# Two groups of layer 2 gathered ahead, its seeds and two ranges fetched inside layer 1, and the SBUF pools laid out in another order

## The chip, the cores and the metric

The kernel runs on one core of a Trainium2 chip. The metric is the device time of one execution in microseconds (us); lower is better. Five engines work side by side, each through its own instructions in the order in which they were written: TensorE (PE, with its weight loads as PEld), VectorE (DVE), ScalarE (ACT), GpSimd (POOL) and SyncE (SP). An instruction that waits holds up everything behind it on its engine. SP, ACT and POOL also issue the DMA transfers, so a transfer that must wait for its buffer holds up the later transfers of the same engine.

## The reference

A graph network of two layers over 6250 nodes with 256 features and 100000 edges, then a residual and a layer norm. The edges are sorted by `dst`, and `dst` is skewed to low numbers.

```python
def _gin_agg(h, src, dst, eps, n_nodes):
    agg = jax.ops.segment_sum(h[src], dst, num_segments=n_nodes)
    return (1.0 + eps) * h + agg
...
h = _gin_agg(x, src, dst, eps1, n)          # 256 wide
h = jax.nn.relu(h @ W1a + b1a)              # 256 -> 512
h = jax.nn.relu(h @ W1b + b1b)              # 512 -> 512
h = _gin_agg(h, src, dst, eps2, n)          # 512 wide
h = jax.nn.relu(h @ W2a + b2a)              # 512 -> 512
out = h @ W2b + b2b                         # 512 -> 256
...
x = _layernorm(x + out, axis=-1)
```

## The kernel before

Nodes are cut into 49 tiles of 128 rows (`t`, the last with 106), edges into 782 chunks of 128. The output of layer 1, called `h` in the profile (`h1` in the code), goes to DRAM and is read again by layer 2.

**Two ways to aggregate.** The seven lowest tiles (0 to 6, "heavy") receive the first 288 chunks. For them the kernel counts how often each node feeds each heavy node (`counting`, L1680, L1712, L1897), and multiplies these counts by the features, one *range* of four tiles after another: in layer 1 by `first_products` (L1606), in layer 2 by `second_products`. There a range `r` is read from `h` into `xr` (L1307), split on ACT and DVE into two parts (`upper` L1362, L1363, L1367), its counts are read from DRAM into `ci` (L1387), cast into `cf` by ACT (L1399), and PE multiplies (L1470: eight matmuls of 512 columns for each of seven heavy tiles). There are 13 ranges; the last has only tile 48. The sums collect in `whole_acc`.

The other 494 chunks belong to 85 *groups* of up to 16 chunks. A group's chunks are gathered row by row: one indirect DMA on POOL for each chunk (L488), 128 rows at a time, into one of six *pieces* of four chunks (layer 2: three in `early`, three in `late`). PE adds them up with a selection matrix (L1066), ACT and DVE split the sum (L1108, L1110), PE spreads it over 128 rows (L1119), and DVE adds it into the accumulators of the tiles that the group reaches (L1129). Piece `i` takes the place of piece `i - 6`, so its gathers wait for that piece's L1066.

**Dense part.** When all of a tile's parts are in, it is turned (L1165, L1177) and multiplied by the two weight matrices (L1204, ACT L1214, L1233). Layer 1 then adds the bias (L1243), applies relu (L1245) and stores to `h` (L1246, from ACT). Layer 2 adds the residual, normalises and stores (L1255 to L1285). An accumulator starts as a scaled copy of the tile's own rows, its seed (`seeding`, L1307, L916).

**The order.** Everything is written out once by a small simulator in the kernel (`Plan`): processes ask for an engine with a cost and a priority (a lower number goes first), for a buffer, or for an event, and the order in which the requests are granted is the instruction order of each engine. Layer 1's instructions stand ahead of layer 2's on every engine. `orders` gives the groups: layer 1 runs from the highest group down; tiles 7 and 6 are its last ones.

**The seam of the layers.** Tiles 6 and 7 (`LATE`) are the last to be stored. Layer 2 therefore begins with a group (`FORE`, group 1, twelve chunks) whose gathers read only the rows of `h` ahead of those two tiles; edges that come from tiles 6 and 7 are pointed at an empty row, and `late_edges` counts them and adds them later by two products of counts and rows (L982 to L1008, L1029, the rows in `sown`). All further gathers read the whole of `h` and wait until it is stored. One range (tile 48 alone) of layer 2's products is done inside layer 1, from when the counting is over (`AHEAD2 = 1`).

**Buffers.** SBUF pools are opened one after the other. Layer 1: `first`, `keep1`, `loan1` and `last1`; layer 2: `keep2` and `loan2` in the same place, once the others are closed. A tile of layer 2 waits for the last user of the layer-1 tile whose place it takes. Layer 2's weights (L735 to L737) are the first tiles of `loan2`, and `fetch()` is called at the head of layer 2's program.

The functions that the change touches follow.

Of the kernel before, what the change touches and what calls it, by code (L numbers as in the profile page):

```python
# [17 lines left out]
P = 128  # L18
EPS_LN = 1e-5
GRP = 20  # L20
PARTS = 4
# [25 lines left out]
PASS = 0.00042  # L47
LATE = (6, 8)
HASTE = -14.0
AHEAD2 = 1  # L50
ACCS2 = 4
AFTER = 4.0
# [300 lines left out]
def tile_gin_residual_layernorm(  # L353
# [115 lines left out]
    FORE0, FOREN = groups[FORE][0], len(members[FORE])  # L469
# [7 lines left out]
    def gather(number, i, table, width, *places):  # L477
# [7 lines left out]
        if number == 2 and pieces[number][i][0] == FORE:  # L485
            table, rows_in, first = h1[: GAP + 1, :], fore, FORE0
# [254 lines left out]
    def rows(t):  # L741
        return min(P, N - t * P)
# [25 lines left out]
    def ordered(ctx):  # L768
# [17 lines left out]

        def layer(number, pools, table, width, scale, weights, ba, wide, at=None, aside=None, right=None):
# [5 lines left out]
            keep, loan, last_ = pools  # L793
# [14 lines left out]
            def reach(g):  # L808

                return range(lo[g] if once or SAME else max(lo[g], tiles), hi[g] + 1)  # L810

            last_use, uses = {}, {t: 0 for t in range(NT)}
            for k, g in enumerate(order):
                for t in reach(g):
                    last_use[t] = k
                    uses[t] += 1
            heavy = range(tiles)
            blocks, taken = [], None
            for t in reversed(range(NT)):
                single = last_use.get(t, -1) >= len(order) - ENDING  # L820
                if taken and not single and len(taken) < TILES and (t >= tiles or (tiles - 1 - t) % TILES):
                    taken.insert(0, t)
                else:
                    taken = [t]
                    blocks.append(taken)
                    if single:
                        taken = None
# [22 lines left out]
            def fetch_rows(i):  # L850
                nonlocal pool_free
                if i < len(pieces[number]):
# [5 lines left out]
                    plan.at(pool_free + LANDINGS[number - 1], arrived[i].set)  # L858

# [4 lines left out]
                keep, [P, 2, width], F32 if once else F32R, "split", SPLITS if once else 3  # L864
            )
            zt_room = Tiles(keep, [P, kk, TILES * P], F32, "zt", 2)
            ht_room = Tiles(keep, [P, KH, TILES * P], F32, "ht", 2)
            if once:
                h_room = Tiles(keep, [P, H], F32, "h1r", 3)
            acc_room = Tiles(  # L870
                keep if once else loan, [P, TILES, width], F32, "acc", ACCS if once else ACCS2
            )
            if not once:
                r_room = Tiles(loan, [P, TILES, D], F32, "r", 2)
                mv_room = Tiles(loan, [P, TILES, 2], F32, "mv", 2)
                st_room = Tiles(loan, [P, 6], F32, "st", 3)
                sd_room = Tiles(loan, [P, TILES], F32, "sd", 2)
                rs_room = Tiles(loan, [P, TILES], F32, "rs", 2)

            if not once:  # L880
                apart = loan.tile([P, len(reach(FORE)), width], F32, name="apart")
                assert all(len(blocks[block_of[t]]) == 1 for t in reach(FORE))

            def seeding(bs, want):
                for i, b in enumerate(bs):
# [5 lines left out]
                    if not once and ts[0] in reach(FORE):  # L891
                        token = Place()
                        token.tile = apart[:, ts[0] - lo[FORE] :]
                    else:
                        token = yield ("get", acc_room, 0)
                    a = token.tile
# [1325 lines left out]
```

## Time and profile before

| | |
|---|---|
| median of 3 runs | 1317.04 us (1312.97 to 1320.39) |
| the profiled execution | 1315.43 us, of which the span of its instructions 1313.6 us |
| instructions | 18937 |
| POOL | 955.4 us busy, 73% of the span |
| moved by DMA | 306.27 MB |

The profile is one execution. A row of the timeline has the start in us, the duration, the engine, the line and the operation, tiles written and read, the count, and in brackets the idle time of the engine ahead of it and what ended it. A row of the groups by line has the count, the busy time and the mean in ns of one, and then the engine's idle time before these instructions with what ended it. A row of the chain of waits has start, duration and what the end was waiting for in that time. A row of windows has, for one stretch, the busy time of each engine, the granted PE clock, and the busy share and rate of the DMA engines. "issue" is idle time for which the profile shows no wait.

### The profile page before, as it was taken

Reading aid. Unit: us, or ns where it says so; the run is one execution under the profiler, and the core shown is the slowest. Engines: PE = TensorE matmul, PEld = TensorE weight load, DVE = VectorE, ACT = ScalarE, POOL = GpSimd, SP = SyncE. Lnnn points to the kernel's source line nnn. Section 1 sums busy time; section 2 is a strip of 40 time slices with the busy share of each in tenths; the row PEclk is TensorE's granted clock in tenths of the full one; section 3 lists DMA queues with packets and bytes.
Section 4 is the critical chain, followed back from the end, with each engine's and each line's share of the span. In section 5 each row is a group of like instructions: output and inputs, shape, how many; then the busy total and the mean of one; then the engine's idle time right before and its main releaser. Section 6 shows DMA issues by size and latency. Waiting matters only on the chain.

```text
span 1313.6 us, 18937 instructions
## 1 busy us (share of the span) xinstructions
PE 1183.7 (90%) x6117; PEld 760.0 (58%) x6117; DVE 874.6 (67%) x2070; ACT 619.8 (47%) x1137; POOL 955.4 (73%) x1001
## 2 busy tenths in 40 slices
PE   6869889999898899779859998999899999999986
PEld 4435455555554455345426676777677667677666
DVE  7978986877886776653147877777666665563343
ACT  6217777575657652464254444344244444242212
POOL 6777777777777777777567777777777777777760
PEclk9879999999999999987879999999999999999999
DMA  6446677666667765575889989788889899877771
GB/s 217 149 131 207 203 210 223 183 202 214 204 201 215 223 197 156 172 227 169 257 293 321 326 252 324 238 301 277 301 254 309 292 308 311 281 234 237 240 229 39
DMA packets 161072, 306.27 MB, mean 233 GB/s; under 512 B 25625, under 2 KB 93103, under 8 KB 160964
## 3 DMA queue, kind: packets, MB, share of 16 engines
q0 software_dynamic: 63232, 194.31, 48.0%
q1 hardware_dynamic: 76778, 86.19, 19.9%
q10 hardware_dynamic: 20954, 24.45, 5.2%
q8 instruction: 52, 0.85, 0.3%
q14 instruction: 56, 0.46, 0.1%
HBM read 274.42 MB, written 30.44 MB: 232 GB/s over the span
## 4 chain that ended last, share of the span: by engine, by line
PE 46%; DMA 16%; DVE 12%; POOL 10%; issue 8%; ACT 6%; ACTq 1%; DVEq 1%; SPq 0%; POOLq 0%
PE bank L1204 12%; POOL early L488 9%; PE bank L1233 9%; PE bank L1066 8%; PE bank L1470 8%; DMA early<-in_x_dram,srcs 5%; PE bank L1119 3%; DMA early<-h,places 3%; PE bank L1606 3%; DVE acc L1129 3%; DVE at L1897 2%; DMA late<-h,places 2%; DMA sown<-h 2%; PE bank L1165 2%; PE bank L1712 1%
## 5 line engine op out<-in xcount | busy, mean ns | idle before, releaser
L488 POOL DMA_INDIRECT early<-in_x_dram,srcs x494 | 480.9, 973 | 153.8 <-issue 128.8
L488 POOL DMA_INDIRECT late<-h,places x242 | 232.6, 961 | 79.6 <-issue 60.3
L488 POOL DMA_INDIRECT early<-h,places x240 | 228.6, 952 | 73.1 <-issue 59.7
L1129 DVE SCALAR_TENSOR_TENSOR acc<-bank,mask,acc 128x256 f32<-128x256 f32 (+1 forms) x360 | 206.6, 606 | 65.0 <-PE bank L1119 58.3
L1233 PE MATMUL bank<-w1b_s,ht 128*128 128x512 f32 (+1 forms) x392 | 184.5, 595 | 2.0 <-ACT ht L1214 1.4
L1204 PE MATMUL bank<-zt,w2a_s 128*128 128x256 f32 (+2 forms) x896 | 181.7, 356 | 3.6 <-ACT zt L1177 2.4
L1066 PE MATMUL bank<-early,sel 128*32 128x256 f32 (+1 forms) x1492 | 139.6, 485 | 40.2 <-DMA early<-in_x_dram,srcs 24.4
L1204 PEld LDWEIGHTS bank<-zt,w2a_s 128*128 128x128 f32 x896 | 154.2, 192 | 33.3 <-issue 8.4
L1470 PE MATMUL bank<-upper,cf 128*128 128x512 f32 (+1 forms) x343 | 148.4, 433 | 0.0
L1470 PE MATMUL bank<-xr,cf 128*128 128x512 f32 (+1 forms) x343 | 136.5, 398 | 0.0
L1897 DVE TENSOR_TENSOR at<-bank,at 128x490 f32 x174 | 116.0, 667 | 25.5 <-ACT cf L1555 13.7
L940 DVE TENSOR_TENSOR sel<-iota,slot 128x256 f32<-128x256 f32 (+3 forms) x116 | 50.9, 439 | 106.0 <-PE bank L1066 98.8
L1119 PE MATMUL bank<-split,to 128*128 128x256 f32 (+2 forms) x340 | 105.7, 430 | 10.4 <-ACT split L1100 4.1
L1214 ACT ACTIVATE ht<-bank,b2a_s 128x256 f32<-128x256 f32 (+2 forms) x112 | 44.6, 443 | 147.9 <-PE bank L1204 144.8
L1066 PEld LDWEIGHTS bank<-early,sel 128*32 128x32 f32 x1492 | 39.5, 113 | 127.6 <-issue 85.3
L1233 PEld LDWEIGHTS bank<-w1b_s,ht 128*128 128x128 f32 (+1 forms) x392 | 72.7, 189 | 67.8 <-issue 54.1
L1606 PE MATMUL bank<-xh,cf 128*128 128x512 f32 (+1 forms) x343 | 100.6, 429 | 11.6 <-DVE xh L1534 10.3
L1399 ACT CAST cf<-ci 128x512 fp32r<-128x512 uint16 (+1 forms) x91 | 54.1, 595 | 116.9 <-PE bank L1470 95.0
L1204 PE MATMUL bank<-zt,w1a_s 128*128 128x256 f32 (+2 forms) x432 | 102.4, 386 | 5.4 <-ACT zt L1177 1.7
L1712 PE MATMUL bank<-cb,ca 128*128 128x490 f16 x288 | 89.0, 386 | 14.3 <-DVE at L1897 5.3
L1680 DVE TENSOR_SCALAR cb<-numbers,spot 128x490 f16<-128x490 f16 x288 | 91.2, 358 | 15.7 <-PE bank L1712 15.5
L1233 PE MATMUL bank<-w2b_s,ht 128*128 128x256 f32 (+1 forms) x392 | 100.0, 386 | 0.0
(176 smaller groups left out, 1692.2 us busy)
## 6 DMA issues: line engine op xcount, KB each, us to landing
raw<-in_x_dram SPq DMA_DIRECT2D x48, 512.0 KB
h<-h1r ACTq DMA_DIRECT2D x48, 256.0 KB
xr<-h SPq DMA_DIRECT2D x11, 1024.0 KB
counts<-ci ACTq DMA_DIRECT2D x84, 128.0 KB
ci<-counts SPq DMA_DIRECT2D x84, 128.0 KB
acc<-h SPq DMA_DIRECT2D x18, 512.0 KB
early<-in_x_dram,srcs POOLq DMA_INDIRECT x494
acc<-in_x_dram SPq DMA_DIRECT2D x21, 256.0 KB
```

The costliest lines, as they stand in the source:

```text
L488: nc.gpsimd.indirect_dma_start(out=rows_[:, j, :], out_offset=None, in_=table, in_offset=bass.IndirectOffsetOnAxis(ap=rows_in[:, c - first ...
L1066: mm = nc.tensor.matmul(pm[b * SLOTS : (b + 1) * SLOTS], sel[:, c - groups[g][0], :], rows_[:, l, :], start=(c == part[0]), stop=(c == par ...
L1119: nc.tensor.matmul(pu[:, i * width : (i + 1) * width], to[:used], split[:used, l, :], start=(once or l == 0), stop=(once or l == 1),)
L1129: nc.vector.scalar_tensor_tensor(acc[t], pu[:, i * width : (i + 1) * width], mask[:, t - lo[g], g : g + 1], acc[t], op0=ALU.mult, op1=ALU.add,
L1204: nc.tensor.matmul(ph[:, (f - o) * TILES * P : (f - o) * TILES * P + nb], wa[:, k, f * P : (f + 1) * P], zt[:, k, :nb], start=(k == 0), st ...
L1233: nc.tensor.matmul(po[:m], ht[:, f, i * P : i * P + m], wb[:, f, :], start=(f == 0), stop=(f == KH - 1),)
L1399: nc.scalar.copy(cf_token.tile[:, :n, :].rearrange("p k j -> p (k j)"), token.tile[:, : n * P],)
L1470: nc.tensor.matmul(bank[token.number][:, :width], cf[:m, j, :], of[:m, j, :], start=(j == 0 and of is upper), stop=(j == len(ks) - 1 and o ...
L1606: nc.tensor.matmul(bank[tokens[i].number][:, : 2 * width], cf[:m, j, :], xh[:m, j, :, :].rearrange("p a d -> p (a d)"), start=(k == 0), st ...
L1680: made = nc.vector.tensor_scalar(token.tile, numbers, spot[:, c : c + 1], None, op0=ALU.is_equal)
L1712: mm = nc.tensor.matmul(bank[token.number][:, : NT * W], a.tile[:, c % BATCH, :], b.tile, start=(j == 0), stop=(j == n - 1),)
L1897: nc.vector.tensor_tensor(to, bank[token[0].number][:, : NT * W].rearrange("p (k w) -> p k w", w=W), to, op=ALU.add,)
```

## The change

1. `FORES` takes the place of `FORE`: the first two groups that reach no lower than tile 7 (groups 1 and 2, twelve chunks each, both reaching tiles 7 and 8) are gathered first, from the rows ahead of tiles 6 and 7. `late_edges` runs once for each; `late_rows` fetches tiles 6 and 7 once for both. Its count is now twelve matmuls of 256 columns, a copy, two turns on PE and a second copy, where it was 24 of 32 columns and one copy.
2. `AHEAD2 = 2`: the range of tiles 44 to 47 joins tile 48's inside layer 1. From the planned landing of layer 1's last gather less 1.5 us (`quiet`) until its last dense matmul (`settled`), no new step of this work is granted (`busy`).
3. `first_seeds` reads the seeds of layer 2's first four blocks (`acc2`, now on the right side of SBUF with `whole_acc`) 8 us after the counting is over, and scales them inside layer 1 at the lowest priority. `ci2` has five buffers in place of six.
4. The pools are `first`, `leave`, `hold`, `keep`, `loan` in layer 1, and `leave`, `hold`, `keep` in layer 2. Layer 2's weights and residual tiles stand in `leave2`; `split`, `zt`, `ht` and `apart` in `hold2`; `late`, `sel`, `to`, `cf` and `sown` in `keep2`.
5. Layer 2's weights are fetched at the planned time 5.0 (`SOWN2`) instead of at the head of its program, and `HASTE`, the planned start of its gathers, goes from -14 to -18.

```diff
+SOWN2 = 5.0
+LEAD = 1.5
-HASTE = -14.0
-AHEAD2 = 1
+HASTE = -18.0
+AHEAD2 = 2
+SOW = 8.0
...
-    FORE = next(g for g in range(BEGIN[1], NG) if lo[g] >= max(HEAVY[1], LATE[0]))
+    FORES = [g for g in range(BEGIN[1], NG) if lo[g] >= max(HEAVY[1], LATE[0])][:2]
+    FORETOLD = range(min(lo[g] for g in FORES), max(hi[g] for g in FORES) + 1)
-    orders[2] = [FORE] + [g for g in reversed(range(BEGIN[1], NG)) if g != FORE]
+    orders[2] = FORES + [g for g in reversed(range(BEGIN[1], NG)) if g not in FORES]
...
-        if number == 2 and pieces[number][i][0] == FORE:
+        if number == 2 and pieces[number][i][0] in FORES:
             table, rows_in, first = h1[: GAP + 1, :], fore, FORE0
...
+            quiet, settled, finished = [], Event(plan), []
+
+            def busy():
+                return once and quiet and plan.now >= quiet[0] and not settled.done
...
+                    if once and i == len(pieces[number]) - 1:
+                        quiet.append(pool_free + LANDINGS[number - 1] - LEAD)
...
+            def first_seeds():
+                yield ("rest", SOW)
...
+                for ts in some[:ACCS2]:
+                    for t in ts:
+                        yield ("until", stored[t])
+                    a = begun_with["pool"].tile(
+                        [P, TILES, H], F32, tag="acc2", name="acc2", bufs=ACCS2
+                    )
+                    in_rows(ts, a, h1, place)
...
+                yield ("rest", SEEDS[1])
+                for ts, a in todo:
+                    if busy():
+                        yield ("until", settled)
+                    yield ("on", "ACT", act(len(ts) * H), 6)
...
-                for part in range(PARTS):
-                    yield ("on", "PE", 0.12 * T * h, 1)
-                    for j in range(T):
-                        for i in range(part, n, PARTS):
-                            nc.tensor.matmul(
-                                ap[:, j * P + part * SLOTS : j * P + (part + 1) * SLOTS],
-                                hot[i][:, j * P : (j + 1) * P],
-                                sel[:, members[FORE][i][0] - FORE0, :],
-                                start=(i < PARTS), stop=(i >= n - PARTS),
-                            )
+                yield ("on", "PE", 0.3 + 0.04 * n, 1)
+                for i, (c, part) in enumerate(members[g]):
+                    nc.tensor.matmul(
+                        ap[part * SLOTS : (part + 1) * SLOTS, : T * P], sel[:, c - c0, :], hot[i],
+                        start=(i < PARTS), stop=(i >= n - PARTS),
+                    )
+                flat = b[:, : 2 * T * P].bitcast(F32)
+                yield ("on", "ACT", act(T * P), 1)
+                nc.scalar.copy(flat, ap[:, : T * P])
...
+                for j in range(T):
+                    nc.tensor.transpose(
+                        ap[:, j * P : (j + 1) * P], flat[:, j * P : (j + 1) * P], ident
+                    )
...
+            def late_rows():
                 yield ("rest", max(0.0, 1.0 - plan.now))
-                s_token = yield ("get", sown["room"], 0)
-                in_rows(range(*LATE), s_token.tile, h1, place)
+                token = yield ("get", sown["room"], 0)
+                in_rows(range(*LATE), token.tile, h1, place)
...
+                    finished.append(t)
+                    if len(finished) == NT:
+                        plan.then(settled.set)
...
-            cf_room = Tiles(loan, [P, RANGE, P], F32R, "cf", 4)
+            cf_room = Tiles(loan if once else keep, [P, RANGE, P], F32R, "cf", 4)
...
-                ci_room = Tiles(pool2, [P, RANGE * P], mybir.dt.uint16, "ci2", 6)
+                ci_room = Tiles(pool2, [P, RANGE * P], mybir.dt.uint16, "ci2", 5)
...
+                            if busy():
+                                yield ("until", settled)
                             token = yield ("get", banks, first or 3)
                             yield ("on", "PE", 2 * PASS * len(ks) * width, first or 3)
...
                     second_products(list(reversed(range(len(ranges))))[:AHEAD2])
+                    plan.start(first_seeds())
...
             def fetching():
-                yield ("rest", WEIGHTS)
+                yield ("rest", WEIGHTS if once else SOWN2 - plan.now)
                 fetch()
...
-            pool = [
+            first, leave, hold, keep, loan = (
                 inner.enter_context(tc.tile_pool(name=name, bufs=1))
-                for name in ("first", "keep1", "loan1")
-            ]
+                for name in ("first", "leave1", "hold1", "keep1", "loan1")
+            )
...
-            pool = [
-                inner.enter_context(tc.tile_pool(name=name, bufs=1)) for name in ("keep2", "loan2")
-            ]
-            layer(2, (*pool, None), h1[:, :], H, e1[:, 1:2], second(pool[1]), b2a_s, D)
+            leave, hold, keep = (
+                inner.enter_context(tc.tile_pool(name=name, bufs=1))
+                for name in ("leave2", "hold2", "keep2")
+            )
```

More of the change, by code (lines that the diff above doesn't have):

```diff
@@ L468, in tile_gin_residual_layernorm @@
     }
-    FORE0, FOREN = groups[FORE][0], len(members[FORE])
+    FORE0 = groups[FORES[0]][0]
+    FOREN = sum(len(members[g]) for g in FORES)
+    assert all(len(members[g]) == PARTS * groups[g][1] for g in FORES)
     places2 = const.tile([P, NCP - NC2], I32, name="places2")
@@ L785, in ordered, with layout, reach @@
         begun_with = {}
+        def layout(number):
+            tiles, order = HEAVY[number - 1], orders[number]
+            def reach(g):
+                return range(lo[g] if number == 1 or SAME else max(lo[g], tiles), hi[g] + 1)
+            last_use, uses = {}, {t: 0 for t in range(NT)}
+            for k, g in enumerate(order):
+                for t in reach(g):
+                    last_use[t] = k
+                    uses[t] += 1
+            blocks, taken = [], None
+            for t in reversed(range(NT)):
+                single = last_use.get(t, -1) >= len(order) - ENDING
+                if taken and not single and len(taken) < TILES and (t >= tiles or (tiles - 1 - t) % TILES):
+                    taken.insert(0, t)
+                else:
+                    taken = [t]
+                    blocks.append(taken)
+                    if single:
+                        taken = None
+            return reach, uses, blocks
         def layer(number, pools, table, width, scale, weights, ba, wide, at=None, aside=None, right=None):
@@ L792, in layer @@
             late_ = not once
-            keep, loan, last_ = pools
+            keep, loan, last_, hold, leave = pools
             wa, wb, bias, fetch = weights
@@ L806, in __init__ @@
                     self.make = lambda: pool.tile(shape, dtype, tag=name, name=name, bufs=bufs)
[L808 to L816, printed above, removed]
-            heavy = range(tiles)
[L818 to L827, printed above, removed]
+            reach, uses, blocks = layout(number)
+            heavy = range(tiles)
             block_of = {t: b for b, ts in enumerate(blocks) for t in ts}
@@ L890, in seeding @@
                         yield ("until", want[b])
-                    if not once and ts[0] in reach(FORE):
+                    if not once and ts[0] in FORETOLD:
                         token = Place()
-                        token.tile = apart[:, ts[0] - lo[FORE] :]
+                        token.tile = apart[:, ts[0] - FORETOLD[0] :]
                     else:
@@ L896, in seeding @@
                     a = token.tile
+                    if not once and begun_with["seeds"] and begun_with["seeds"][0][0] == ts:
+                        begun_with["seeds"].pop(0)
+                        held[b] = token
+                        for i, t in enumerate(ts):
+                            acc[t] = a[:, i, :]
+                            ready[t].set()
+                        settle(ts[0])
+                        continue
                     where = natural if once else place
@@ L1032, in adding_late @@
                     )
-                for token in tokens:
-                    token.release()
+                counts_token.release()
+                sown["late"].used()
                 plan.then(plan.start, then)
@@ L1069, in sums @@
                                 start=(c == part[0]),
-                                stop=(c == part[-1] and (once or g != FORE)),
+                                stop=(c == part[-1] and (once or g not in FORES)),
                             )
@@ L1397, in converting @@
                     cf_token = yield ("get", cf_room, 0)
+                    if busy():
+                        yield ("until", settled)
                     yield ("on", "ACT", act(n * P), first or 3)
@@ L1462, in multiplying @@
                             yield ("until", halved[r])
+                            if busy():
+                                yield ("until", settled)
                             token = yield ("get", banks, first or 3)
```

104 lines of the change are left out of this document (69 added, 35 removed).

## The prediction, made before the result was known

> **What bounds the kernel now.** I read the page's engine shares first, then windows along the span, then the gathers in the groups by line.
>
> ```profile
> PE 1183.7 (90%) x6117; PEld 760.0 (58%) x6117; DVE 874.6 (67%) x2070; ACT 619.8 (47%) x1137; POOL 955.4 (73%) x1001
> core 0: us, PE busy (x) PEld busy (x) DVE busy (x) ACT busy (x) POOL busy (x), PEclk, DMA share, GB/s
> 600.00:640.00 40.00, 38.40 (x189) 21.54 (x187) 10.30 (x20) 17.33 (x42) 28.38 (x31) 0.90 0.55 167
> 640.00:661.00 21.00, 15.91 (x62) 9.76 (x62) 1.57 (x3) 4.78 (x13) 9.46 (x10) 0.76 1.00 325
> 661.00:675.00 14.00, 0.63 (x8) 0.36 (x8) 6.79 (x24) 10.52 (x16) 6.25 (x6) 0.68 0.65 204
> 675.00:1200.00 525.00, 512.61 (x2724) 358.84 (x2726) 346.69 (x680) 215.95 (x404) 398.22 (x417) 0.98 0.88 289
> 1200.00:1281.00 81.00, 75.13 (x456) 53.59 (x449) 35.10 (x84) 16.11 (x38) 58.63 (x62) 1.00 0.77 229
> L488 POOL DMA_INDIRECT late<-h,places x242 | 232.6, 961 | 79.6 <-issue 60.3 <-DMA h<-h1r 6.2 <-DMA late<-h,places 5.8
> L488 POOL DMA_INDIRECT early<-h,places x240 | 228.6, 952 | 73.1 <-issue 59.7 <-DMA early<-h,places 7.3 <-PE bank L1066 2.1
> ```
>
> By share PE is the bound. But PE has the products of counts to fill its time with; POOL has nothing but gathers, and its 482 gathers (242 + 240) took 461.2 us with 152.7 us between them, of which only the 6.2 us behind `DMA h<-h1r` are one long wait: the rest is 0.3 us a gather. So from its start on POOL runs at its own pace, and PE's work fits under it. POOL's timeline shows it:
>
> ```profile
> 648.55 0.95 POOL L488 DMA_INDIRECT early<-h,fore  x1 [11.04 <-DMA acc<-h]
> 662.31 0.95 POOL L488 DMA_INDIRECT early<-h,fore  x1 [0.30 <-issue]
> 669.48 1.01 POOL L488 DMA_INDIRECT late<-h,places  x1 [6.22 <-DMA h<-h1r]
> 685.06 0.95 POOL L488 DMA_INDIRECT early<-h,places  x1 [0.30 <-DMA late<-h,places]
> 1276.26 0.95 POOL L488 DMA_INDIRECT late<-h,places  x1 [0.30 <-issue]
> ```
>
> Twelve gathers lie from 648.55 to 662.31, 1.25 us apart; then POOL stands still until tiles 6 and 7 are stored; the 25th gather starts at 685.06, the last at 1276.26. Ahead of 648.55 it idled 11 us for the store of tile 8. Layer 2's end is therefore that start, plus 494 gathers, plus the waits, plus the 37.3 us from 1276.26 to the span's end at 1313.6. A microsecond taken out of POOL's start or its one wait comes off the end, as long as PE keeps up.
>
> **The change part by part.** The sum is made against the profiled execution, 1315.4 us (span 1313.6), which is 1.6 us under the median.
>
> *Second group ahead.* Twelve more gathers no longer ask for tiles 6 and 7. The 25th then starts at 648.55 + 24 x 1.253 = 678.6 instead of 685.06: **-6.4**. The whole of `h` is there by then:
>
> ```profile
> 662.52 6.19 DMA h<-h1r
> 668.90 0.56 DVE L940 TENSOR_TENSOR sel<-iota,slot 128x384 f32<-128x384 f32 x1 [7.08 <-DMA h<-h1r]
> 675.24 5.02 PE L1066 MATMUL bank<-early,sel 128*32 128x512 f32 x24
> 690.95 1.13 PE L1029 MATMUL bank<-sown,zt 128*128 128x512 f32 x2
> 693.79 1.02 PE L1029 MATMUL bank<-sown,zt 128*128 128x512 f32 x2
> ```
>
> The store lands at 662.52 + 6.19 = 668.7. What is late next is the place: the 25th gather takes the first group's first piece, which L1066 freed at 675.24 + 5.02 = 680.3. That matmul waited for `sel`, whose DVE stood 7.08 us behind the store because `sel` lay where layer 1's buffers had been. With the new pools DVE can begin when the last dense matmul ends, near 661, so L1066 should be through by about 673. The price is a second count and 1.13 + 1.02 = 2.2 us of L1029 on PE, hidden under POOL's pace; uncovered it would cost 2.2 plus about 1 us of short matmuls.
>
> *Range 44 to 47 and the seeds.* Seven groups of eight L1470 matmuls leave layer 2:
>
> ```profile
> 747.40 1.87 PE bank L1470 x8
> L1399 ACT CAST cf<-ci 128x512 fp32r<-128x512 uint16 x84 | 51.9, 619 | 115.4 <-PE bank L1470 95.0 <-DMA ci<-counts 9.4 <-issue 6.2
> 662.97 3.23 ACT L916 ACTIVATE acc<-acc,e 128x1024 f32<-128x1024 f32 x3 [0.48 <-ACT h1r L1245]
> ```
>
> 7 x 1.87 = 13.1 us of PE, seven casts x 0.619 = 4.3 us of ACT (77 of 84 remain). Between 600 and 640 PE was idle only 1.6 of 40 us; between 661 and 675 it did 0.63 us in 14. So I expect one to three of the seven ahead of layer 1's end and the rest behind its last dense matmul, where PE stood idle. By itself this takes nothing off POOL's chain (0); it lets PE enter layer 2 some 10 us less behind. The seeds' scaling (3.23 us and one more) leaves an ACT that was not late: 0.
>
> *Layer 1's end.* Here transfers decide:
>
> ```profile
> 311.11 3.46 DMA early<-in_x_dram,srcs
> 636.57 7.26 DMA early<-in_x_dram,srcs
> 634.13 0.38 SPq L735 DMA_DIRECT2D w2a_s<-in_L_gnn_W2a_dram  x1
> 640.56 0.33 ACTq L1246 DMA_DIRECT2D h<-h1r  x1
> 643.97 1.08 PE L1066 MATMUL bank<-early,sel 128*32 128x256 f32 x8 [4.26 <-DMA early<-in_x_dram,srcs]
> 647.71 0.25 SPq L1312 DMA_DIRECT2D acc<-h  x1
> q1 hardware_dynamic: 2795, 3.90, 79.6%
> q0 software_dynamic: 225, 0.59, 11.5%
> ```
>
> The last gather of layer 1 needed 7.26 us, where an undisturbed one took 3.46, and PE idled 4.26 us for it; tile 8's store, which starts layer 2's gathers, took from 640.56 to 647.7. In this stretch (634 to 650, the two queue rows) SP's queue moved 3.90 MB, the weights among them from 634.13 on, and the gathers 0.59. The change moves the weights past the seam and range and seeds ahead of it; what SP still issues here is the next range's rows. A landing like the 3.46 would bring the start forward by 3.7 us (7.1 - 3.46). On the other side each product that slips ahead of tile 8's dense work costs 1.9. Bounds -4 and +4; I take **-2**, since the weights (1.7 MB by their shapes) leave this stretch, but SP's order is not known.
>
> The Trainium skill, "DMA: Bandwidth & Descriptors", section "Queues, rings and completion order", says that each DMA engine serves its queues in turn, a packet at a time. This speaks against putting another range and the seeds beside layer 1's last forty microseconds of gathers; the trace agrees that a full SP queue roughly doubles a landing (7.26 against 3.46). By this rule alone, with SP's queue as full as before at 636, the term would be 0 instead of -2 and the time 1308, still inside the forecast's band below.
>
> *Pools.* `late` may now wait. By the tiles' sizes in the code, the last third of `late` and a strip of the middle lie where layer 1's `cf` was, and `cf` is used until the last product of range 44 to 47. The 17th gather is due at 668.6 and the 21st at 673.6; five products behind 661 end near 661 + 9.4 = 670.4. Nothing to 6.4 us; I take **+0.5**, the trace showing PE and ACT free there.
>
> *Tail.*
>
> ```profile
> 1277.67 0.60 PE L1165 MATMUL bank<-ident,acc 128*128 128x128 f32 x4
> 1281.41 1.07 PE L1066 MATMUL bank<-late,sel 128*32 128x512 f32 x8
> 1291.79 0.60 PE L1165 MATMUL bank<-ident,whole_acc 128*128 128x128 f32 x4
> 1295.01 0.60 PE L1165 MATMUL bank<-ident,apart 128*128 128x128 f32 x4
> L1129 DVE SCALAR_TENSOR_TENSOR apart<-bank,mask,apart x7: 719/743/752, 699.8 to 1285.6; 128x512 f32<-128x512 f32 x7
> ```
>
> The last sum is added by 1285.6 + 0.74 = 1286.3, yet the last two tiles are turned at 1291.79 and 1295.01, because PE is still at the two tiles before them. Now group 2 is out of the way, tiles 8 and 9 are complete with group 3, sixteen gathers (20 us) before the last. At best 1291.8 - 1286.3 = 5.5 us go. PE was idle only 5.9 of 81 us from 1200 to 1281, so most of the queue is real: I take **-1.5**; bounds -5.5 and 0.
>
> The sum: -6.4 - 2 + 0.5 - 1.5 = -9.4, so 1315.4 - 9.4 = **1306.0**.
>
> **The rivals.**
>
> ```profile
> L1362 ACT CAST upper<-xr 128x512 fp32r<-128x512 f32 x48 | 29.6, 617 | 2.9 <-DMA xr<-h 2.9
> L1363 ACT COPY bank<-xr 128x512 f32<-128x512 f32 x48 | 28.1, 585 | 1.6 <-DVE xr L1367 0.9 <-DVE acc L1129 0.6
> ```
>
> *The wait moves into `late` (no change).* If most of the range is held back until `settled`, with its splitting on ACT, products run until about 661 + 4.8 + 13.1 = 679 (four tiles at 0.617 + 0.585 us, then seven products). Gathers 21 to 24 start there, the 25th near 684, and L1066 comes behind. The 6.4 is given back and 2 to 4 us remain: about 1312. This is also the case in which the change does not do what its words say, the range not being done when counting is over. For it: PE had 1.6 us free before 640. Against it: the products need only 13 us and the casts four buffers.
>
> *Layer 1 is pushed back (slower).* Low-priority products are not interrupted once granted. If PE takes all seven between 600 and 640, 13.1 less the 1.6 idle, tile 8's store and the gathers start 11.5 us later: -6.4 + 11.5 = +5.1, 1320.5. It decides from a delay of 6.4 us on, that is from about four products ahead of tile 8's matmuls. For it: PE full in that window. Against it: the work has the lowest priority, and a hold 1.5 us before the last landing.
>
> *PE's relief counts too (faster).* Landing and tail both at their good ends: -6.4 - 4 - 5.5 = -15.9, 1299.5. For it: the tail queue on PE; against it: the written order fixes PE's waits whatever it has free.
>
> **How the numbers follow.** Forecast (1302 to 1310) 0.48; moved wait 0.22; slower 0.12; relief 0.18. The likeliest gives 1306.0. The range reaches from below the third rival to the middle of the second, 1298 to 1318; the three runs of before lie 7.4 us apart, too. A difference under 0.5% (6.6 us) cannot be told from none: below 1310.5 lie most of the forecast and all the relief, 0.60; within 0.5% the moved wait and the forecast's upper edge, 0.28; slower 0.12.
>
> **What would show it.** POOL's wait on `h<-h1r` gone, 24 `fore` gathers in a row, the 25th near 675 to 679, the last near 1268; about 77 casts behind the seam; landing of layer 1's last gather under 6 us; L1066 of group 1 before 675. I am wrong if POOL waits for PE or ACT near 668 to 680, if tile 8's store comes after 643, or if the end does not follow POOL's last gather by about 36 us.

## The result, and the profile after

The change made the kernel slower: 1329.44 us median of four runs (1328.54 to 1330.58) against 1318.33 (1312.97 to 1320.39), a ratio of 1.0086 with a 95% interval of 1.0062 to 1.0109. The prediction, 1306.0 within 1298 to 1318, was wrong in its sign. The profiled execution took 1330.58 us, its span 1328.8, 15.2 more than before's; the medians lie 11.1 apart. All points of time below come from one profiled execution of each kernel. One run of all that follow, the tenth of one_haste18, took 2365.57 us and counts neither in its kernel's median nor in its ratio.

The engine line of the page of after:

```profile
PE 1189.1 (89%) x6125; PEld 763.8 (57%) x6125; DVE 878.8 (66%) x2085; ACT 621.0 (47%) x1140; POOL 959.0 (72%) x1001
```

PE has 5.4 us more work than before and POOL 3.6: no engine's work explains 15 us. POOL's timeline of after, at the points that were shown of before (start, duration, engine, line, operation, and in brackets the idle time ahead of it with its releaser):

```profile
639.81 0.94 POOL L494 DMA_INDIRECT early<-in_x_dram,srcs  x1 [0.30 <-issue]
667.04 0.95 POOL L494 DMA_INDIRECT early<-h,fore  x1 [26.29 <-PE bank L1282]
...
682.44 1.17 POOL L494 DMA_INDIRECT late<-h,fore  x1 [0.30 <-ACT bank L1446]
683.92 1.43 POOL L494 DMA_INDIRECT late<-h,fore  x1 [0.30 <-issue]
...
698.17 0.95 POOL L494 DMA_INDIRECT early<-h,places  x1 [0.30 <-issue]
...
1289.58 0.95 POOL L494 DMA_INDIRECT late<-h,places  x1 [0.30 <-issue]
```

The wait of 6.22 us for `h<-h1r` is gone, and 24 `fore` gathers stand in a row, as was meant. But the first of them starts at 667.04 instead of 648.55, 18.5 us later, after POOL has idled 26.3 us until tile 8 was stored (the row names matmuls of PE that end near that time; the store itself is shown below). From there the distances are: to the 25th gather 31.1 us (36.5 before), to the last 622.5 (627.7 before), and 39.2 from it to the span's end (37.3 before). So +18.5 at the seam, -5.2 in layer 2's gathers, +1.9 in the tail: +15.2.

What made the seam late stands in the timeline of after between 604 and 627, SP's queue first:

```profile
604.08 0.43 SPq L1388 DMA_DIRECT2D acc<-h  x1
...
606.17 1.48 SPq L1388 DMA_DIRECT2D acc<-h  x3
607.74 1.43 SPq L1393 DMA_DIRECT2D raw<-in_x_dram  x1
609.22 7.58 SPq L1388 DMA_DIRECT2D xr<-h  x1
...
625.48 0.40 ACT L1612 CAST xh<-raw 106x256 fp32r<-106x256 f32 x1 [9.23 <-DMA raw<-in_x_dram]
...
626.67 0.79 PE L1694 MATMUL bank<-xh,cf 106*128 106x512 f32 x1 [8.73 <-DVE xh L1621]
```

The last piece of `x` that layer 1 itself still needs (`raw`, 106 rows) is issued at 607.74, behind the seeds (`acc<-h`), and ACT gets it at 625.48, 17.7 us later, having waited 9.23 us; PE idles 8.73. In before no seeds stood ahead of it:

```profile
603.40 0.29 SPq L1312 DMA_DIRECT2D raw<-in_x_dram  x1
...
614.35 0.43 ACT L1525 CAST xh<-raw 106x256 fp32r<-106x256 f32 x1
```

Issued at 603.40, it was taken at 614.35 with no wait at all. The kernel one_range, described below, has the seeds in the same place but not the second range, and shows the same delay, 17.4 us:

```profile
609.85 0.96 SPq L1393 DMA_DIRECT2D raw<-in_x_dram  x1
...
627.29 0.40 ACT L1612 CAST xh<-raw 106x256 fp32r<-106x256 f32 x1 [13.81 <-DMA raw<-in_x_dram]
```

The second delay follows it, between 645 and 673 in after's timeline:

```profile
645.97 0.40 PE L1557 MATMUL bank<-upper,cf 128*128 128x512 f32 x1
...
648.70 0.48 PE L1557 MATMUL bank<-upper,cf 128*128 128x512 f32 x1
...
650.65 1.05 PE L1282 MATMUL bank<-zt,w1a_s 128*128 128x128 f32 x8
...
651.46 0.48 PE L1557 MATMUL bank<-upper,cf 128*128 128x512 f32 x1
...
654.98 0.48 PE L1557 MATMUL bank<-upper,cf 128*128 128x512 f32 x1
...
663.19 0.33 ACTq L1327 DMA_DIRECT2D h<-h1r  x1
...
672.55 0.79 PE L1557 MATMUL bank<-upper,cf 128*128 128x512 f32 x1
```

These are the first matmuls of four groups of eight, products of range 44 to 47, lying between the gathers' matmuls and the dense work of the last tiles. PE is already late there and does them nevertheless, since their place in its order is written; the other three come behind tile 8's store, from 672.55. The store is issued at 663.19 instead of 640.56. Its landing, on the other hand, became quick: 663.19 to POOL's start at 667.04 is 3.9 us, where it had been 640.56 to 648.55, 8.0.

### The profile page after: what moved, and what is told of

Its sections match the earlier page's. It is cut to its first block, busy times and chain, and to the rows that moved or that the text cites. A ratio compares the mean times of both kernels' runs of the same rounds, so it can differ in the third digit from the quotient of the medians.

```text
span 1328.8 us, 18986 instructions
## 1 busy us (share of the span) xinstructions
PE 1189.1 (89%) x6125; PEld 763.8 (57%) x6125; DVE 878.8 (66%) x2085; ACT 621.0 (47%) x1140; POOL 959.0 (72%) x1001
## 5 line engine op out<-in xcount | busy, mean ns | idle before, releaser
L494 POOL DMA_INDIRECT late<-h,places x232 | 222.2, 958 | 70.7 <-issue 61.3
L1282 PE MATMUL bank<-zt,w2a_s 128*128 128x256 f32 (+2 forms) x896 | 184.7, 361 | 5.2 <-ACT zt L1255 4.2
L1694 PE MATMUL bank<-xh,cf 128*128 128x512 f32 (+1 forms) x343 | 104.4, 442 | 19.0 <-DVE xh L1621 18.6
L1197 PE MATMUL bank<-split,to 128*128 128x256 f32 (+3 forms) x340 | 102.1, 419 | 14.2 <-DVE split L1188 4.5
L1002 DVE TENSOR_TENSOR sel<-iota,slot 128x256 f32<-128x256 f32 (+2 forms) x116 | 50.8, 438 | 87.9 <-PE bank L1144 87.4
L1768 DVE TENSOR_SCALAR cb<-numbers,spot 128x490 f16<-128x490 f16 x288 | 90.9, 357 | 22.8 <-PE bank L1800 22.6
L1621 DVE TENSOR_TENSOR xh<-bank,xh 128x512 fp32r<-128x512 f32 (+1 forms) x100 | 67.1, 673 | 48.6 <-ACT bank L1619 48.2
```

The costliest lines, as they stand in the source:

```text
L494: nc.gpsimd.indirect_dma_start(out=rows_[:, j, :], out_offset=None, in_=table, in_offset=bass.IndirectOffsetOnAxis(ap=rows_in[:, c - first ...
L1197: nc.tensor.matmul(pu[:, i * width : (i + 1) * width], to[:used], split[:used, l, :], start=(once or l == 0), stop=(once or l == 1),)
L1282: nc.tensor.matmul(ph[:, (f - o) * TILES * P : (f - o) * TILES * P + nb], wa[:, k, f * P : (f + 1) * P], zt[:, k, :nb], start=(k == 0), st ...
L1621: nc.vector.tensor_tensor(xh[:m, two, 1, :], ap, xh[:m, two, 0, :], op=ALU.subtract)
L1694: nc.tensor.matmul(bank[tokens[i].number][:, : 2 * width], cf[:m, j, :], xh[:m, j, :, :].rearrange("p a d -> p (a d)"), start=(k == 0), st ...
L1768: made = nc.vector.tensor_scalar(token.tile, numbers, spot[:, c : c + 1], None, op0=ALU.is_equal)
```

## The experiments

Three theories were set against each other. **A**: layer 1's end is pushed back, by the seeds ahead of `raw` in SP's queue and by the products ahead of tile 8; without these POOL's gain reaches the end. **B**: the second group and the new pools cost more than they bring. **C**: the additional transfers disturb the seam wherever they stand. All edits are made to the kernel after the change. The times in the text are of the profiled executions; ratios are to the kernel before, run on the same chip. "Fore" is the start of the first gather of layer 2, and the tail the time from the start of the last gather to the span's end.

*Without the early seeds.*

```diff
-                    plan.start(first_seeds())
+                    begun_with["seeds"] = []
```

> The changed kernel without the early seeds: they are read in layer 2's program, as before; the second range stays inside layer 1. Theory A (layer 1's end is pushed back: by the seeds, which SP issues ahead of the last piece of x for first_products, and by the products of range 44 to 47 ahead of tile 8's dense matmuls): PE's idle time of 8.7 us behind 617.9 goes, the products remain, the first fore gather starts near 657 instead of 667 and the time is about 1319. Theory B (the new pools, or the second group's count, cost the time): the first gather may move, but the time stays at 1326 or more. Theory C (any extra bytes beside the gathers cost it, in whatever order): about half, 1323 to 1326.

*One range in layer 1, as before, with the seeds.*

```diff
-AHEAD2 = 2
+AHEAD2 = 1
```

> The changed kernel with only tile 48's range inside layer 1 (as before) and the early seeds kept. Theory A: the 8.7 us of PE idle time for the last piece of x stay, the four product groups of 1.9 us ahead of tile 8's dense matmuls go; first fore gather near 659, time about 1321. Theory B: 1326 or more. Theory C: 1322 to 1326.

*Both edits: no early seeds and one range.*

> The changed kernel with neither the early seeds nor the second range: what is left is the new pools, the second group ahead and the later fetch of the weights. Theory A: both delays go, the first fore gather starts at 645 to 649 and the 25th near 676 to 679, time 1305 to 1310, faster than before. Theory B: 1322 or more. Theory C: about 1315, as before.

*The seeds kept, with both ranges, but later.* 22 us after the counting instead of 8; SP then issues them behind `raw`.

```diff
-SOW = 8.0
+SOW = 22.0
```

> The changed kernel with the seeds' planned time 22 us after the end of counting instead of 8, so that SP issues the last piece of x ahead of them; the same bytes in the same layer. Theory A: that piece lands within 6 to 8 us instead of 17.7, PE's idle time of 8.7 us is gone or under 2; the products stay; first fore gather 657 to 660, time about 1320. Theory C: 1327 or more, since the bytes are the same. Theory B: 1327 or more.

Measured, with the first fore gather, the 25th, the last and the tail, in us:

| kernel | fore | 25th | last | tail | median | ratio (95%) |
|---|---|---|---|---|---|---|
| before | 648.55 | 685.06 | 1276.26 | 37.3 | 1318.33 | 1 |
| after | 667.04 | 698.17 | 1289.58 | 39.2 | 1329.44 | 1.0086 (1.0062 to 1.0109) |
| no_seeds | 648.30 | 685.46 | 1282.37 | 42.2 | 1326.32 | 1.0080 (1.0050 to 1.0110) |
| one_range | 658.88 | 689.43 | 1281.00 | 40.2 | 1329.00 | 1.0083 (1.0051 to 1.0115) |
| neither | 647.23 | 677.83 | 1277.77 | 40.6 | 1319.65 | 1.0022 (1.0004 to 1.0040) |
| seeds_later | 652.89 | 689.84 | 1281.08 | 40.7 | 1323.61 | 1.0066 (1.0042 to 1.0091) |

(one_range's seven runs lie between 1319.56 and 1329.88, its profiled one, 1322.97, near the lower end: three runs at a mean granted clock of 0.964 to 0.966 took 1323 or less, four at 0.957 to 0.959 took 1329 or more.)

For the seam A is right: each part alone brings the start back, the seeds' order by 14 us (seeds_later), one range less by 8, the seeds' absence by 19. But A had said that the end follows, and it doesn't. Its times, about 1319, 1321, 1305 to 1310 and 1320, stand against medians of 1326.32, 1329.00, 1319.65 and 1323.61. The first two are where B had them (1326 or more), the other two lie between A and B. no_seeds starts as early as the kernel before and is still slower. Its timeline on POOL, and the end of the range's products on PE:

```profile
648.30 0.95 POOL L494 DMA_INDIRECT early<-h,fore  x1 [7.01 <-DVE acc L1207]
...
668.77 0.40 PE L1557 MATMUL bank<-xr,cf 128*128 128x512 f32 x1
669.91 0.95 POOL L494 DMA_INDIRECT late<-h,fore  x1 [6.91 <-issue]
```

The 13th gather is the first into `late`; it waits 6.91 us, and starts 0.7 us after the last product of range 44 to 47 has ended at 669.17. The releaser is not named in the row. In seeds_later it is, and there two rows ahead of the seam show one more wait:

```profile
634.66 1.15 ACT L966 ACTIVATE acc<-acc,e 128x1024 f32<-128x1024 f32 x1 [2.04 <-DMA acc<-h]
...
637.15 2.08 PE L1282 MATMUL bank<-zt,w1a_s 128*128 128x128 f32 x8 [3.13 <-ACT zt L1255]
...
652.89 0.94 POOL L494 DMA_INDIRECT early<-h,fore  x1 [13.49 <-DVE acc L1207]
...
673.16 0.40 PE L1557 MATMUL bank<-xr,cf 128*128 128x512 f32 x1
674.30 0.95 POOL L494 DMA_INDIRECT late<-h,fore  x1 [6.71 <-ACT cf L1484]
```

`late` lies where layer 1's `cf` was, and has to wait for the products that were held back until `settled`. The two rows ahead of it belong to the seeds: ACT stands still until they land, so as to scale them (2.04 us here, 3.14 for the seeds before these), and PE waits 3.13 us for the copy behind that scaling. So the seeds still cost the seam something in seeds_later: tile 8's store is issued at 649.83, in no_seeds at 645.44. With one range (the kernel neither) the wait of `late` is gone and the 25th gather stands at 677.83, but POOL waits later, for PE:

```profile
647.23 0.95 POOL L494 DMA_INDIRECT early<-h,fore  x1 [7.41 <-PE bank L1243]
...
707.24 0.94 POOL L494 DMA_INDIRECT early<-h,places  x1 [2.21 <-PE bank L1144]
...
759.88 1.01 POOL L494 DMA_INDIRECT late<-h,places  x1 [7.32 <-PE bank L1144]
```

9.5 us are lost by 760: POOL waits there for PE to free the places of `early` and `late`. And this kernel is not one without these transfers in layer 1's time: its seeds belong to layer 2's program, but SP issues them long before the seam, since their place is free:

```profile
616.80 0.42 SPq L1388 DMA_DIRECT2D acc<-h  x1
```

C is answered below, by a kernel that moves the same seeds in layer 1 and starts earliest of all.

*Two groups without new pools, one group with them.* In two_groups the pools and the weights' place are as before, there is one range and there are no early seeds, but two groups go ahead; `HASTE` stays at -18. In pools_only the new pools stand, with one group ahead and `HASTE` at -14, as before. The core of two_groups:

```diff
-AHEAD2 = 2
+AHEAD2 = 1
...
-            cf_room = Tiles(loan if once else keep, [P, RANGE, P], F32R, "cf", 4)
+            cf_room = Tiles(loan, [P, RANGE, P], F32R, "cf", 4)
...
-                    plan.start(first_seeds())
+                    begun_with["seeds"] = []
...
-                2, (keep, None, None, hold, leave), h1[:, :], H, e1[:, 1:2], second(leave),
+                2, (keep, loan, None, keep, loan), h1[:, :], H, e1[:, 1:2], second(loan),
```

and pools_only:

```diff
-HASTE = -18.0
-AHEAD2 = 2
+HASTE = -14.0
+AHEAD2 = 1
...
-    FORES = [g for g in range(BEGIN[1], NG) if lo[g] >= max(HEAVY[1], LATE[0])][:2]
+    FORES = [g for g in range(BEGIN[1], NG) if lo[g] >= max(HEAVY[1], LATE[0])][:1]
...
-                    plan.start(first_seeds())
+                    begun_with["seeds"] = []
```

> The kernel before with the second group ahead and nothing else of weight: the old pools, the weights fetched at the head of layer 2, one range and no early seeds. Theory A (the second group takes the wait of 6.2 us out of POOL's chain, and what POOL gains is given back where the rows in sown land late): 24 fore gathers in a row from about 648.5, the 25th at 678 to 680, 6 us earlier than before; then new waits of POOL for the places of pieces, 5 to 9 us in all, last gather near 1275, time 1314 to 1319. Theory B (the gain holds, and it was the new pools that gave it back in the run without seeds and second range): no new waits, last gather near 1270, time 1307 to 1311.

> The new pools and the later fetch of the weights, with one group ahead, one range, no early seeds. Theory A: the wait for the store of tiles 6 and 7 is back (about 6 us), the landing at layer 1's end is short, first fore gather near 647, 25th near 683; no or little waiting behind it, since POOL is as late as before; time 1313 to 1317. Theory B: POOL waits in the first 100 us of layer 2 also here, 5 us or more, and the time is 1318 or more.

*Two groups and one group with one range, the seeds behind `raw`.* one_range_later:

```diff
-AHEAD2 = 2
+AHEAD2 = 1
-SOW = 8.0
+SOW = 22.0
```

pools_one_later has, besides these:

```diff
-HASTE = -18.0
+HASTE = -14.0
...
-    FORES = [g for g in range(BEGIN[1], NG) if lo[g] >= max(HEAVY[1], LATE[0])][:2]
+    FORES = [g for g in range(BEGIN[1], NG) if lo[g] >= max(HEAVY[1], LATE[0])][:1]
```

> The changed kernel with only tile 48's range inside layer 1 and the seeds asked for 22 us after the end of counting instead of 8. Theory A (seam): the last piece of x is ahead of the seeds, no product stands ahead of tile 8, so the first fore gather starts at 646 to 650 and the 25th at 677 to 680; with 2 MB of seeds no longer read behind the seam the rows in sown land sooner, POOL waits under 4 us behind it, last gather 1268 to 1273, time 1309 to 1314. Theory B (the new pools cost): POOL waits 8 us or more and the time is 1319 or more.

> As the run before, with one group ahead instead of two. Theory A: 25th gather near 683, last near 1275, time 1313 to 1318, some 4 us over the run with two groups. If the second group is worth nothing once layer 2's start is bound by its transfers, both take the same time within 1.5 us.

| kernel | fore | 25th | last | tail | median | ratio (95%) |
|---|---|---|---|---|---|---|
| two_groups | 645.88 | 682.90 | 1275.96 | 42.5 | 1319.88 | 1.0029 (1.0018 to 1.0041) |
| pools_only | 644.54 | 677.54 | 1271.06 | 39.6 | 1316.18 | 0.9997 (0.9981 to 1.0013) |
| one_range_later | 643.28 | 674.26 | 1270.03 | 41.1 | 1316.71 | 1.0020 (0.9997 to 1.0043) |
| pools_one_later | 644.28 | 679.96 | 1271.64 | 35.4 | 1307.99 | 0.9938 (0.9916 to 0.9959) |

Against theory A's times, two_groups and one_range_later came out a little late (1314 to 1319 and 1309 to 1314 were expected), pools_only within them.

**pools_one_later beats both kernels**, by more than its expectation had (1313 to 1318): new pools and seeds in layer 1, but one group ahead, one range, and the seeds issued behind `raw`. one_range_later differs from one_range in the seeds' planned time alone; its timeline shows that it is the order of the queue, not the bytes, that made `raw` late:

```profile
602.52 0.26 SPq L1393 DMA_DIRECT2D raw<-in_x_dram  x1
...
606.68 0.43 SPq L1388 DMA_DIRECT2D acc<-h  x1
...
610.36 0.43 ACT L1612 CAST xh<-raw 106x256 fp32r<-106x256 f32 x1
...
643.28 0.94 POOL L494 DMA_INDIRECT early<-h,fore  x1 [5.56 <-PE bank L1243]
...
750.65 1.01 POOL L494 DMA_INDIRECT late<-h,places  x1 [3.60 <-PE bank L1144]
```

The seeds leave at 606.7, within 3 us of the place that they have in after, and tile 8's store is issued at 640.42, in before at 640.56: here they cost the seam nothing, and C, by which the bytes disturb it in whatever order, falls. What they cost in seeds_later came by ACT's wait. In two_groups the second group brings POOL nothing (the 25th gather, expected at 678 to 680, comes at 682.90). With the old pools the first gather into `late` waits for layer 1's last store, whose rows it doesn't read, so presumably for its place:

```profile
645.88 0.94 POOL L494 DMA_INDIRECT early<-h,fore  x1 [7.58 <-DMA ci<-counts]
...
667.23 1.00 POOL L494 DMA_INDIRECT late<-h,fore  x1 [6.67 <-DMA h<-h1r]
```

one_range_later, where only the 3.60 us at 750 are left of such waits, has POOL's last gather 1.6 us ahead of pools_one_later and ends 4.1 us later: the tail is 5.7 us longer. Two causes of that were tried: that with two groups PE carries layer 2 (**P**, against **Q**, that POOL's cadence carries it), and that `HASTE` writes another order.

*Less work on PE.* In two of layer 2's ranges the products are made from `xr` alone; the kernels leave out those with `upper`:

```diff
-                                for of in (upper, xr):
+                                ofs = (xr,) if not once and r in (4, 8) else (upper, xr)
+                                for of in ofs:
...
-                                        start=(j == 0 and of is upper),
+                                        start=(j == 0 and of is ofs[0]),
```

> one_range_later (two groups ahead, one range and the seeds in layer 1, seeds late) with the products of two of layer 2's ranges made from xr alone: 2 x 7 x 4 matmuls from upper, 0.43 us each, about 24 us less of PE, are left out; the order and all else stay. What is left out is the upper part of two of the eleven ranges of products. Theory P (with two groups PE, not POOL, carries layer 2: between tile 8's store and the end it idled only 39.5 of 670.7 us in one_range_later, and its tail after POOL's last gather is a queue on PE): the tail falls from 41.1 us to about 36, the end by 5 to 8 us, to a profiled span of 1303 to 1306 and a median near 1309. Theory Q (POOL's cadence carries it, and the tail is set by the written order's waits): the last gather stays at 1270 +-1, the span at 1311 +-1.5.

> pools_one_later (one group ahead) with the same 24 us of PE's products left out (the upper part of two of the eleven ranges). Theory P: with one group POOL and PE are nearly level (tail 35.4 us, no queue seen in it), so it gains less than the kernel with two groups: 0 to 3 us, span 1304 to 1307. Theory Q: no gain, span 1307 +-1.5, last gather 1271.6 +-1.

*HASTE alone*, exchanged between the two kernels: -14 in one_range_later (two_haste14), -18 in pools_one_later (one_haste18).

> one_range_later with HASTE at -14 as before (the planned time of layer 2's first gather), two groups still ahead. If the longer tail of two groups (41.1 against 35.4 us) comes from the order that HASTE -18 writes, the tail falls to 35 to 37 us and the median to 1309 to 1311. If it comes from the second group's work (theory P), the tail stays at 40 to 42 us and the median within 3 us of 1316.7.

> pools_one_later with HASTE at -18, one group ahead. If the order that HASTE writes makes the tail, the tail rises from 35.4 us to 39 to 42 and the median from 1308.0 to 1312 to 1316. If the second group makes it (theory P), the tail stays at 35 to 37 us and the median within 2.5 us of 1308.0.

| kernel | fore | 25th | last | tail | median | ratio (95%) |
|---|---|---|---|---|---|---|
| two_light | 646.69 | 677.41 | 1273.01 | 40.9 | 1318.09 | 0.9995 (0.9976 to 1.0015) |
| one_light | 644.51 | 679.53 | 1271.14 | 34.7 | 1309.75 | 0.9947 (0.9921 to 0.9972) |
| two_haste14 | 644.66 | 676.01 | 1277.17 | 41.1 | 1323.59 | 1.0038 (1.0015 to 1.0060) |
| one_haste18 | 645.87 | 682.33 | 1274.43 | 36.7 | 1316.84 | 0.9983 (0.9964 to 1.0002) |

P falls by the traces. Between tile 8's store and the end PE had 631.17 us of work in one_range_later and 618.44 in two_light; its idle time rose from 39.5 to 51.7 us instead, and neither the way from the first fore gather to the last (626.8 and 626.3 us) nor the tail (41.1 and 40.9) moved. (The edit took 12.7 us from PE, not the 24 that its expectation names: the rows of single matmuls overlap, and eight of them take 1.87 us.) The ratios alone would not decide it: 1.0020 and 0.9995 have intervals that overlap, and leave room for the 2.6 to 4.2 us that P's 5 to 8 for 24 us of work come to for 12.7. With one group they are 0.9938 and 0.9947. The tail goes with the work that stands behind the last gather in PE's written order, and with the waits written into it. In the windows from the last gather to the end (window, length, PE busy with its count of matmuls, granted clock, share of the DMA engines, GB/s), first one_range_later, then two_light, pools_one_later, one_light, after and two_haste14:

```profile
1270.03:1311.10 41.07, 30.38 (x214) 0.93 0.18 55
```

```profile
1273.01:1313.90 40.89, 30.38 (x214) 0.93 0.17 55
```

```profile
1271.64:1307.00 35.36, 24.59 (x182) 0.94 0.19 60
```

```profile
1271.14:1305.80 34.66, 24.50 (x182) 0.90 0.19 60
```

```profile
1289.58:1328.80 39.22, 26.78 (x186) 0.87 0.18 56
```

```profile
1277.17:1318.30 41.13, 27.87 (x198) 0.95 0.17 54
```

From one_range_later to pools_one_later it is 32 matmuls fewer behind the last gather, 5.8 us less of PE, and a tail shorter by 5.7. Products left out earlier change nothing there. But work alone is not all of it: two_haste14 has 198 matmuls and the tail of 214, since PE idles 13.3 us in it instead of 10.7. Four kernels differ in groups and `HASTE` alone. At -14 one group is faster by 1.0% (0.9938 against 1.0038), at -18 the two are not told apart (0.9983 against 1.0020, intervals that overlap, and both profiled spans 1311.1): there the two groups' last gather comes 4.4 us sooner and their tail is 4.4 us longer. So B is right in that the second group brings nothing in any of these, and wrong of the pools: pools_only equals the kernel before, and pools_one_later stands on the same pools. `HASTE` does not make the long tail: it stays at 41.1 us with two groups, and goes from 35.4 to 36.7 with one, as the two expectations had it for the second group. Their times both came out higher (1323.59 and 1316.84). two_haste14 loses ahead of the tail, where 632.5 us pass from the first fore gather to the last. Over all 14 kernels the tail is 39.2 to 42.5 us in the nine with two groups, and 34.7 to 39.6 in the five with one. What stays open is how the planner comes to write one tail or the other: the tails were read from the traces, not derived from the code. `HASTE` moves the time by 0.45% with one group and not measurably with two. The medians of pools_one_later and pools_only lie 8.2 us apart; of these the profiled pair shows 3.7, all in the tail. So moving the seeds gained time there, but the runs do not show how.

## Why the prediction was wrong, step by step

- **Layer 1's end, -2 with bounds -4 and +4: the step that failed.** It measured +18.5. The landing was right: the store's way to POOL's start fell from 8.0 to 3.9 us, the good bound (2.9 in the kernels no_seeds and neither). The windows row of after for this stretch (length, busy time of PE, PEld, DVE, ACT and POOL, granted clock, DMA share, GB/s) shows why:

```profile
640.00:663.00 23.00, 22.14 (x115) 13.56 (x114) 7.38 (x14) 11.70 (x25) 0.75 (x1) 1.00 0.37 114
```

  The transfers are at a share of 0.37 where before's row from 640 to 661 has 1.00. The Trainium skill, "DMA: Bandwidth & Descriptors", section "Queues, rings and completion order", whose rule of queues served in turn was weighed in the prediction, agrees: the landing shortens where the other queues are empty. But the store's issue moved by +22.6, and the upper bound counted products alone: for a load of layer 1 that waits in SP's queue behind the seeds the step had nothing. Beside one_range_later, whose store is issued at 640.42, one_range shows the seeds' order alone (656.01, +15.6). After has 22.8; the 7.2 that are left fit the four groups of products ahead of tile 8's matmuls, 4 x 1.87 = 7.5. The price of the range is not fixed: in no_seeds only one such group stands there, and the store is at 645.44, +5.0 (+1.1 beside the kernel neither, 644.37).
- **Range and seeds at 0 on POOL's chain.** Wrong by the same figures. The text said that SP's order was not known and then priced the seeds by ACT's scaling only, and that at 0; seeds_later shows ACT standing still for their landing. The row of `raw` at 603.40 was in before's trace: a queue that still carried something layer 1 needed, into which the change put the seeds at about that time.
- **The rival that layer 1 is pushed back** had the sign (1320.5, chance 0.12), half of the mechanism and too small a price: it needed all seven products ahead of tile 8. Four were there, about 7.5 us, and PE's 8.73 us of waiting for `raw` had no place in it. Its deciding point, 6.4 us, was passed.
- **Second group ahead, -6.4.** Right where it was worked out: from the first fore gather to the 25th 31.1 us instead of 36.5, -5.4. The microsecond that is missing is in four gathers of 1.05 to 1.43 us between 679 and 685. Wrong in what it is worth: "a microsecond taken out of POOL's start or its one wait comes off the end" doesn't hold. From after to no_seeds the start moves by -18.7 and the span by -4.2; in the kernel neither the 25th gather came 7.2 us sooner than before's and the last 1.5 us later. After's gathers ran without waits behind a late start; that they did because of it is likely, but not shown.
- **The wait that moves into `late`**, +0.5 with a rival at 1312. After shows none, only the usual 0.30 us between two gathers; no_seeds and seeds_later show the rival, 6.9 and 6.7 us with the 25th gather at 685.46 and 689.84 (the rival: near 684), but at the 13th gather, the first into `late`, where the step had expected it at the 17th or 21st.
- **Tail, -1.5, bounds -5.5 and 0.** It measured +1.9. PE's timeline of after's tail:

```profile
1289.31 0.66 PE L1243 MATMUL bank<-ident,apart 128*128 128x128 f32 x4
...
1303.97 0.60 PE L1243 MATMUL bank<-ident,whole_acc 128*128 128x128 f32 x4
1304.40 0.60 PE L1243 MATMUL bank<-ident,apart 128*128 128x128 f32 x4
1307.27 9.04 PE L1282 MATMUL bank<-zt,w2a_s 128*128 128x128 f32 x64 [2.27 <-ACT zt L1255]
```

The first tile in `apart` is turned just ahead of the last gather, not 4.6 us after it as in before, and the last two from 14.4 us after the last gather on (15.5 in before): 1.1 us were won, as the step said. But the order now turns both at once: PE waits 2.27 us for ACT's copies, the 64 matmuls behind them take 9.04 us, and from the turn to the end it is 24.8 us instead of 21.8. Part of that is the clock of this one execution: two_haste14 has the same order behind the same wait, takes 7.41 us for the 64 matmuls and 23.6 from the turn to the end. And the step had the sign wrong beyond this pair, since each of the nine kernels with two groups has a tail longer than before's 37.3. The third rival, PE's relief, had this tail as a main gain; what the prediction held against it, that the written order fixes PE's waits, is what happened, the clock aside.
- **The signs named beforehand** served: "if tile 8's store comes after 643" (663.19), and the end following POOL's last gather by 39.2 instead of 36 us.

## What to carry to other kernels

Before work is moved ahead of a seam, list what each queue still carries for the stage that is ending, and put the new transfers behind the last of it: the same seeds held up tile 8's store by 15.6 us ahead of a small load and, with one range, not at all behind it. Ask also which engine will work on what the transfer brings: an instruction that waits for it holds up what stands behind, as ACT's scaling did in seeds_later. Work of low priority that a planner writes into an engine's order is free only if the gap is there at run time; once the engine is late it stands in the way like any other. And where a chain is said to be the bound, ask what would wait next if it started earlier: here the places in `late`, waits for PE and the tail's written order took back what the head had gained.

## What the hardware showed unexpectedly

A load of 106 rows that was issued behind the seeds was taken 17.7 us after its issue, while in one_range_later, issued ahead of the same seeds, it was there for ACT within 7.8 us (602.52 to 610.36, without a wait). The Trainium skill, "DMA: Bandwidth & Descriptors", section "Why a DMA increments its semaphore by 16 and not by 1", says that a load runs on the largest number of engines up to 16 that divides its outermost size, which gives two for 106 rows, and the section "Queues, rings and completion order" that each engine takes a queue's descriptors in order. That would make such a load late behind bulk on the same queue; the runs here show the lateness and its cure by order, but none varied the number of rows.

And 64 matmuls of the same shape behind the same wait of 2.27 us took 9.04 us in after's tail and 7.41 in two_haste14's. Over just these matmuls the traces have a mean granted clock of 0.81 in after, with 0.50 from 1309 to 1312, and of 1.00 in two_haste14; 9.04 x 0.81 = 7.3, so the clock accounts for the difference. Why the same idle time was followed by a lower clock in one execution and not in the other is not shown:

```profile
1297.98 7.41 PE L1282 MATMUL bank<-zt,w2a_s 128*128 128x128 f32 x64 [2.27 <-ACT zt L1255]
```
